# Two-layer graph network with top-p attention: fewer candidates in step two, and the order of the work between the steps

## The chip, the cores and the metric

The kernel runs on one core of a Trainium2 chip. The time is device microseconds of the whole program, so lower is better. Engines are named as in the profile: PE (TensorE, matmuls), DVE (VectorE), ACT (ScalarE), POOL (GpSimd), SP (SyncE, which here only issues DMAs). "L749" is line 749 of the kernel before.

## What is computed

`x` is 2708 x 256 and `adj` 2708 x 2708, with ones in about 0.3% of its places and on its diagonal, each times a number from 0.05 to 1. All is float32. Two layers follow each other:

```python
def adj_layer(x, adj, weight, bias):                  # layer 0
    return relu(concat([x, adj @ x], 1) @ weight + bias)

def top_p(X):                                         # attention of layer 1
    logits = (X @ W1.T @ W2.T) @ (X @ W3.T).T
    probs = softmax(logits)
    # keep, row by row, the largest entries until their sum reaches 0.9
    A = probs * mask
    return A / A.sum(-1)

def layer1(X, S):
    R = S + eye;  R = R / R.sum(-1)
    Z, Xf, Xa = 0, X, X
    for n in range(2):                                # the two steps
        Xf, Xa = R @ Xf, top_p(Xa) @ Xa
        Z = Z + Xf @ U1[n].T + Xa @ U2[n].T
    return layernorm(X + Z) * g + b

x = layernorm(x + adj_layer(x, adj, weight, bias))
x = layernorm(x + layer1(x, adj))
```

## The kernel before, in words

Rows are cut into NB = 22 blocks of 128 (the last, EDGE, has 20). The program has four stages.

**Load and layer 0.** SP loads `xT` in chunks of 512 columns and then the adjacency of block 0. PE makes `y0 = x @ w0` block by block (L392); ACT and DVE copy every other block out of PSUM (L395, L399), and ACT also issues the loads of the weights in between (L397). Then for each of 22 blocks PE multiplies the adjacency with y0 (L257), and DVE does relu and layer norm. DVE also writes down for every block which 128-wide rows of the adjacency hold an entry; sorted lists of these names go through DRAM (`list_d`) and come back as the index tile `ix`, CC = 7 indices for each of 128 lanes and each block. Since a list may be short, the DRAM lists are first filled with the name of an empty row (L279 to L282): an iota writes 154 numbers into `ix` on 128 partitions, and two DMAs of POOL's queue spread them, 28 B a piece.

**Step one.** For each block: logits, exponential, the 64 largest entries in order (`extract1`, candidates from 16 segments of 170 columns), a mask by the threshold, transposes (L527), and the product with x1 (L564). The edge block's product lies in four strips of 32 partitions that `edge_sum` adds with one small matmul (L244). `step1_out` gives three functions that scale the result, turn it (`turn_out`) and project it to the queries and keys of step two and to `za` (`project`, L699).

**Between the steps.** A *y pair* (`ya_pair`, L672 and L675) is four matmuls of two blocks of the turned results with U2, and one copy by ACT into `ya`, through one of the two `acc` buffers of PSUM. There are 11 pairs, and step two's attention products read `ya`. An *R unit* is one matmul (L749) of the product R @ y: 8 units are one R block, 7 with a gathered `y` and one with the block's own rows. `r_units(n)` issues the next n units; when it begins an R block, it also issues the loads of the one after it (`r_load`, SP: adjacency and own rows; POOL: 7 indirect DMAs, L719, into one of two `yg` buffers). A finished R block's `r_out` (L777 in the first half, L792 in the second) is put in a list that is run two slots later. The first half, 22 blocks, reads `yf_d` and writes `v_d`; the second half reads `v_d`. The second half's first gather is issued by the last `r_out` of the first.

**Step two** is a software pipeline of 24 periods, each with six slots g = 0 to 5. In period `per`, DVE searches and cuts: for block `per` it makes `last_level`, one pass over the whole row that keeps what is below the level (`below_level`, L1023), and the eight largest of each segment (`candidates`, L1030, 20 segments of 136); for block `per - 1` it puts the 48 largest candidates in order (`in_order`, L1039 and L1042: MAX8 and MATCH_REPLACE8 in turn), finds the threshold (`threshold`), marks ties (`mark`, four L1083) and cuts the row (`mask`, L1088). ACT makes the exponentials of block `per + 2` (L844, L848) and four passes over block `per + 1` (`try_act`, L966 and L969), whose output goes to a scratch row `scr` that nobody reads. The sums of these passes set the next level by the constants STEPS and FEW. PE turns and multiplies block `per - 2` (L527, L564), makes logits (L507) and the R units that the table `units` gives to the period. `final_slot` does the last layer norms for up to two new blocks and two that had their first norm: `new` ones get their statistics, a slot later are normalized by ACT (L1192) and on POOL multiplied with g and added to x1 (L1207, L1208); they are then `finals` and get their second statistics (L1182). In period 22 and after it the last block ends the program. A sum of flags at the end sends the program through a general path if any row's candidates did not suffice.

The order of the work on each engine is the order in which the Python code issues it. Each engine takes its instructions in that order; an instruction waits until its data are there and its buffer is free, and what stands behind it waits too.

Step two has five rows of exponentials: e0 to e3 are the buffers of step one (`es`), and e4 is half of `tile2`, which takes the place of `xaT_all` (tag "V"), so it can be written only when the last y pair has read that. The other half of `tile2` is `scr`. `tile1` (`low`, `w`) takes the place of x1.

Of the kernel before, what the change touches and what calls it, by code (L numbers as in the profile page):

```python
# [9 lines left out]
FP = mybir.dt.float32  # L10
I32 = mybir.dt.int32
# [9 lines left out]
P = 128  # L21
CH = 512
SEG = 170
NS = 16
SEG2 = 136
NS2 = 20
TOP1 = 64
TOP2 = 48
WS = 4

GUESS = 2.76141059
STEPS = ((0.93339875, 14.44678062, 82.55022771), (0.98700001, 8.00991560, 128.06811957))
FEW = 20.0
TOP_S = 0.8999
TIE_EPS = 1.5e-5
KS = 7
# [1 line left out]
ML = 16  # L40
CW, CC = 128, 7
# [107 lines left out]
def fast_path(ctx, tc, c, flags, fint, xT_d, x_d, w0_d, b0_d, w1_d, w2_d, w3_d, u1_d, u2_d, g_d, b_d):  # L149
    nc = tc.nc  # L150
    N, D, DA, NB, DC, KH, CHS, rows = c.N, c.D, c.DA, c.NB, c.DC, c.KH, c.CHS, c.rows
    ident = c.ident
    adj_d, out_d, x1_d, za_d = c.adj_d, c.out_d, c.x1_d, c.za_d
    NW = SEG * NS
    NF = flags.shape[1]

    big = ctx.enter_context(tc.tile_pool(name="big", bufs=1))
# [11 lines left out]
    def ps_acc(t=None):  # L169
        acc = ps.tile([P, CH], FP, tag="acc", name="acc")  # L170
        if t == NB - 1:
            nc.vector.memset(acc[:, :D + 1], 0.0)
        return acc

    def ps_misc():
        return ps.tile([P, CH], FP, tag="misc", name="misc")
# [56 lines left out]
    fold = small.tile([P, EW], FP, tag="fold", name="fold", bufs=1)  # L233
    nc.vector.tensor_reduce(fold, ident.rearrange("p (j i) -> p i j", i=EW), AX.X, ALU.add)

    def edge_sum(acc, n, stop=True, meanwhile=None):

        p = rows(EDGE)
        four = work.tile([P, 4, P], FP, tag="wT", name="four", bufs=3).rearrange("p k i -> p (k i)")
        nc.scalar.copy(four[:, :n], acc[:, :n])  # L240
        if meanwhile:
            meanwhile()
        whole = ps_misc() if meanwhile else ps_acc()
        nc.tensor.matmul(whole[:p, :n], lhsT=fold[:, :p], rhs=four[:, :n], start=True, stop=stop)  # L244
        return whole

# [18 lines left out]
    LAST = NB * P * NB - 1  # L265
# [11 lines left out]
    for y_d in (c.yf_d, c.v_d):  # L277
        nc.gpsimd.dma_start(out=y_d[rows(NB - 1):, NB - 1, :], in_=zero)
    ix = small.tile([P, NB, CC], I32, tag="ix", name="ix", bufs=1)  # L279
    nc.gpsimd.iota(ix.rearrange("p m c -> p (m c)"), pattern=[[0, NB * CC]], base=LAST, channel_multiplier=0)  # L280
    for i, (a, b) in enumerate(((0, ML), (ML, NB))):
        nc.gpsimd.dma_start(out=c.list_ds[i][:, :CW * CC].rearrange("m (p c) -> p m c", c=CC), in_=ix[:, a:b, :])  # L282
    before_m = small.tile([NB, 1], FP, tag="before_m", name="before_m", bufs=1)
    nc.gpsimd.iota(before_m, pattern=[[0, 1]], base=0, channel_multiplier=KS * CAP,
                   allow_small_or_imprecise_dtypes=True)
# [376 lines left out]
    def ya_pair():  # L662


        if not y_pairs:
            return
        t0 = y_pairs.pop(0)
        pz = ps_acc().rearrange("p (s d) -> p s d", d=D)
        for s in range(2):
            p, at = rows(t0 + s), (t0 + s) * P  # L670
            for j in range(DC):
                nc.tensor.matmul(pz[:p, s, :], lhsT=xaT_all[:, j, at:at + p], rhs=c.u2[:, j, 1, :],  # L672
                                 start=j == 0, stop=j == DC - 1)
        if rows(t0 + 1) == P:
            nc.scalar.copy(ya[:, t0:t0 + 2, :], pz)  # L675
            return
        for s in range(2):
            nc.scalar.copy(ya[:rows(t0 + s), t0 + s, :], pz[:rows(t0 + s), s, :])
# [218 lines left out]
    for t in range(NB):  # L897
        acc = ps_acc(t)
        part = exps1(t + 2) if t + 2 < NB else None
        b = None  # L900
        if t >= NB - 3:
            b = blocks[t - (NB - 3)] = Block(t - (NB - 3))
        ra_next = finish1(t + 1) if t + 1 < NB else None
        for g in range(NG):
            turn(t, g, x1, acc, es[t % 4])
            if ends and 1 <= g <= 3:
                ends[g - 1]()
            if g < NL and t + 3 < NB:
                logits1(t + 3, g)
            if b and g in (0, 2):  # L910
                lg = logits(1, b.t, g // 2)
                if g == 0:
                    shift(b, lg[0])
            if b and g in (1, 3):
                exps2(b, g // 2, *lg)
            if part and g in (3, 4):
                part(g - 3)
            products(1)
            if stores and stores[0][0] <= NG * t + g:
                adj_store(*stores.pop(0)[1:])  # L920
            if g == 2:
                if t + 3 < NB:
                    extract1(t + 3)
                if t < 9:
                    lists.take(2 * t + 2, 2 * t + 4)
                if t == 8:
                    lists.end()
            if (t, g) in at:
                adj_gather(at[t, g])
                stores += [(NG * t + g + i, at[t, g], i - 4) for i in (4, 5)]  # L930
            if (t, g) in y_at:
                name_y()
                y_load(0, y_at[t, g])
            if (t, g) == (NB - 1, 2):
                a_load(0)
        if t == EDGE:
            products(0)
            acc = edge_sum(acc, D, meanwhile=ya_pair)
        ends = step1_out(t, acc, ra)
        ra = ra_next  # L940
    assert not stores and not staged and not to_turn
    r_load(0, 0)
    for f in ends:
        ya_pair()
        f()
    ya_pair()
    for t in range(3):
        exps2(blocks[t], 2, *logits(1, t, 2))
        ya_pair()
    while y_pairs:  # L950
        ya_pair()

    tile1 = big.tile([P, 2 * NW], FP, tag="x1", name="w")
    low = tile1[:, :NW]
    w = tile1[:, NW:]
    tile2 = big.tile([P, 2 * NW], FP, tag="V", name="e4")
    nc.gpsimd.memset(tile2[:, N:NW], 0.0)
    ring.append(tile2[:, :NW])
    scr = tile2[:, NW:]

    def try_act(b, k, part):

# [261 lines left out]
    def final_slot(i):  # L1224


        if i == 2:
            while ready and len(new) < 2:
                new.append(Final(*ready.pop(0)))
                new[-1].load()  # L1230
        if i == 1:
            while done:
                done.pop().store()
        n = len(new) + len(finals)
        if i == 3:
            for k, f in enumerate(new + finals):
                f.stats(k)
        if i == 5 and n:
            roots(0, n)
        if i == 0 and n:  # L1240
            over(0, n)
            for f in finals:
                f.end()
            for f in new:
                f.middle()
            done[:] = finals
            finals[:] = new
            new.clear()
# [3 lines left out]

    each = NB * (CC + 1)
    first = 2 * (CC + 1)
    units = {0: CC + 1, 1: CC + 1}
    rest = each - first - sum(units.values())
    units.update({p: rest * (p - 1) // 8 - rest * (p - 2) // 8 for p in range(2, 10)})
    units.update({p: each * (p - 10) // 11 - each * (p - 11) // 11 for p in range(11, 22)})
    assert first + sum(units.values()) == 2 * each


    b0, b1, b2 = (blocks[t] for t in range(3))
# [7 lines left out]
    try_act(b0, 1, 0)  # L1270
    next_level(b0, 1)
    for per in range(NB + 2):
        if per == NB + 1:
            tail.append(True)
        n_r = units.get(per, 0)
# [8 lines left out]
        for g in range(NG):  # L1284
# [26 lines left out]
            if b_act:  # L1311
                for k, part in {0: ((0, 0),), 1: ((0, 1), (0, 2), (0, 3)), 2: ((1, 0),), 3: ((1, 1), (1, 2), (1, 3))}.get(g, ()):
                    try_act(b_act, k, part)
            next(vector)
            if g == 0:
                final_slot(0)
# [415 lines left out]
```

## Time and profile before

| | |
|---|---|
| median of 3 runs | 1303.6 us (1302.28 to 1304.17) |
| the profiled execution | 1308.28 us, its span 1306.5 us, mean granted clock of PE 0.98 |
| busy: PE, DVE, ACT, POOL | 1236.7, 997.3, 735.6, 641.9 us |
| first adjacency product (L257) of block 0 | 33.2 us |
| last product of step one (L561) | ends at 730.0 us |
| first R unit of step two's stage (L749) | 756.7 us |
| pass L1023 of blocks 0, 1, 2 and 10 | 760.8, 783.7, 794.2, 985.0 us |
| mask L1088 of blocks 20 and 21 | 1267.2, 1282.6 us |

In lines of the timeline the first number is the start in us from the start of the span, the second the duration, then engine, line, operation and what it writes and reads; in brackets stands how long the engine was idle before it, and what released it. In lines of the chain of waits the two numbers are start and duration. A wait that the profile names "issue" has nothing to show for it. PE's instructions appear twice for each matmul of float32 ("x8" is four matmuls), and its busy time is modelled. The granted clock falls to one half in stretches.

### The profile page before, as it was taken

To read this page: it belongs to the slowest core of one execution; us is meant where nothing else is said; L and a number is where in the kernel's file an instruction comes from. 1 tells how busy PE (TensorE), PEld (TensorE's weight loads), DVE (VectorE), ACT (ScalarE), POOL (GpSimd) and SP (SyncE) were. 2 spreads that over 40 slices of the span, in tenths; PEclk is the share of its full clock that TensorE was granted. 3 is DMA by queue.
4 is the path that set the end of the run, shared out by engine and by line. 5 is a ranking of instruction groups with operands and counts; after the bars stand their busy time and mean duration, and the time that the engine had idled before them with its cause. 6 is when DMAs were issued, how large, how long until landed. Compare 5 with 4: busy or idle time off the path is not lost.

```text
span 1306.5 us, 18895 instructions
## 1 busy us (share of the span) xinstructions
PE 1236.7 (95%) x5764; PEld 892.9 (68%) x5764; DVE 997.3 (76%) x3406; ACT 735.6 (56%) x1337; POOL 641.9 (49%) x594
## 2 busy tenths in 40 slices
PE   7999999979899999999999978999999999999975
PEld 5878778843477777777777556777765777766753
DVE  2455445884999997977771279989888999999996
ACT  1010110125456656655665488887888989989821
POOL 1000000002465442577666068878775778888850
PEclk9999999999999999999999888999999999999898
DMA  7455445423322220132324145565663645555551
GB/s 189 152 171 165 149 160 169 148 89 105 119 81 84 70 71 12 40 93 92 91 85 107 49 150 156 177 184 169 185 145 114 197 143 161 175 169 156 151 121 38
DMA packets 101704, 166.00 MB, mean 127 GB/s; under 512 B 17362, under 2 KB 74070, under 8 KB 101594
## 3 DMA queue, kind: packets, MB, share of 16 engines
q1 hardware_dynamic: 75308, 108.65, 26.0%
q0 software_dynamic: 20544, 51.17, 15.1%
q10 hardware_dynamic: 5742, 4.89, 1.4%
q8 instruction: 48, 0.79, 0.3%
q14 instruction: 62, 0.51, 0.1%
HBM read 130.74 MB, written 33.90 MB: 126 GB/s over the span
## 4 chain that ended last, share of the span: by engine, by line
PE 77%; DVE 10%; ACT 6%; DMA 3%; POOL 2%; issue 1%; SPq 0%; ACTq 0%; POOLq 0%; DVEq 0%
PE acc L564 26%; PE acc L257 16%; PE lg L507 9%; PE misc L749 9%; PE tr L527 7%; PE acc L651 2%; DVE e L1088 2%; DVE w L1083 2%; PE acc L462 2%; PE misc L426 2%; PE acc L672 2%; PE misc L699 2%; DMA xT<-in_xT 1%; POOL yg L719 1%; ACT e L844 1%
## 5 line engine op out<-in xcount | busy, mean ns | idle before, releaser
L530 ACT COPY wT<-tr 128x512 f32<-128x512 f32 (+2 forms) x258 | 132.0, 519 | 216.8 <-PE tr L527 215.8
L564 PE MATMUL acc<-x,wT 128*128 128x256 f32 (+1 forms) x924 | 230.5, 388 | 0.0
L564 PE MATMUL acc<-ya,wT 128*128 128x256 f32 (+1 forms) x924 | 228.1, 386 | 0.0
L719 POOL DMA_INDIRECT yg<-v_d,ix x154 | 196.6, 1277 | 59.8 <-issue 23.2
L719 POOL DMA_INDIRECT yg<-yf_d,ix x154 | 191.6, 1244 | 48.3 <-issue 23.1
L564 PEld LDWEIGHTS acc<-x,wT 128*128 128x128 f32 (+1 forms) x924 | 165.2, 189 | 71.0 <-issue 37.4
L257 PE MATMUL acc<-y,adj_t 128*128 128x257 f32 (+1 forms) x924 | 208.4, 381 | 0.0
L564 PEld LDWEIGHTS acc<-ya,wT 128*128 128x128 f32 (+1 forms) x924 | 170.6, 191 | 44.5 <-issue 24.0
L749 PE MATMUL misc<-yg,adj_t 128*128 128x256 f32 (+1 forms) x704 | 185.1, 396 | 14.0 <-DMA yg<-v_d,ix 6.6
L257 PEld LDWEIGHTS acc<-y,adj_t 128*128 128x128 f32 (+1 forms) x924 | 171.8, 189 | 32.7 <-issue 8.9
L367 POOL DMA_INDIRECT adj_t<-in_adj,ix x154 | 167.8, 1089 | 51.8 <-issue 44.1
L749 PEld LDWEIGHTS misc<-yg,adj_t 128*128 128x128 f32 (+1 forms) x704 | 124.2, 191 | 67.2 <-issue 21.5
L507 PE MATMUL lg<-k,q 64*128 64x512 f32 (+3 forms) x528 | 150.2, 596 | 14.0 <-ACT e L848 7.0
L527 PE MATMUL tr<-ident,e 128*128 128x128 f32 (+2 forms) x946 | 148.5, 276 | 7.5 <-DVE e L1088 6.3
L527 PEld LDWEIGHTS tr<-ident,e 128*128 128x128 f32 (+2 forms) x946 | 113.0, 140 | 52.1 <-issue 24.0
L334 POOL DMA_DIRECT2D part_d<-e x1 | 0.6, 573 | 290.3 <-DVE e L333 290.3
L966 ACT ACTIVATE e<-e,st 128x2708 f32<-128x2708 f32 (+1 forms) x43 | 113.5, 2640 | 0.1
L439 ACT COPY x1T<-tr 128x256 f32<-128x256 f32 (+1 forms) x22 | 8.0, 364 | 186.6 <-PE tr L438 186.6
L969 ACT ACTIVATE e<-e,st 128x2708 f32<-128x2708 f32 (+1 forms) x42 | 110.9, 2641 | 0.1
L570 DVE MAX8 cand<-e 128x8 f32<-128x170 f32 (+1 forms) x352 | 87.2, 317 | 26.6 <-ACT e L514 26.6
L1030 DVE MAX8 cand<-w 128x8 f32<-128x136 f32 (+1 forms) x440 | 105.9, 284 | 0.0
L1083 DVE MATCH_REPLACE8 w<-part,e 128x680 f32<-128x680 f32 (+1 forms) x88 | 74.3, 850 | 0.0
(238 smaller groups left out, 1732.3 us busy)
## 6 DMA issues: line engine op xcount, KB each, us to landing
adj_t<-in_adj SPq DMA_DIRECT2D x44, 704.0 KB
adj_t<-adjc_d SPq DMA_DIRECT2D x44, 448.0 KB
adjc_d<-adj_t SPq DMA_DIRECT2D x22, 256.0 KB
base<-za_d SPq DMA_DIRECT2D x40, 128.0 KB
adjc_d<-adj_t SPq DMA_DIRECT2D x22, 192.0 KB
xt<-in_x ACTq DMA_DIRECT2D x21, 128.0 KB
x_d<-x SPq DMA_DIRECT2D x21, 128.0 KB
x1b_d<-xb SPq DMA_DIRECT2D x21, 128.0 KB
```

What stands on the lines that cost most here:

```text
L257: nc.tensor.matmul(acc[:p, :n], lhsT=halves[k // KH][:kw, k % KH, :p], rhs=y[:kw, k, :n], start=k == 0, stop=stop and k == NB - 1)
L367: nc.gpsimd.indirect_dma_start(out=a[:CW, i, :], out_offset=None, in_=adj_rows, in_offset=bass.IndirectOffsetOnAxis(ap=ix[:CW, m, i:i + 1] ...
L507: nc.tensor.matmul(lg[:p, h, :b - a], lhsT=q[o, t * P:t * P + p], rhs=keys[s][o, i, :b - a], start=True, stop=True)
L527: nc.tensor.transpose(tr[:kw, k % 4, :p], e[:p, k * P:k * P + kw], ident[:p, :p])
L530: nc.scalar.copy(wT[:, :full, :p], tr[:, :full, :p])
L564: nc.tensor.matmul(acc[:p, :D], lhsT=wT[:kw, k % 4, :p], rhs=y[:kw, k, :], start=k == 0, stop=k == NB - 1)
L719: nc.gpsimd.indirect_dma_start(out=y[:CW, i, :], out_offset=None, in_=rows_d, in_offset=bass.IndirectOffsetOnAxis(ap=ix[:CW, m, i:i + 1], ...
L749: nc.tensor.matmul(acc[:p, :D], lhsT=a[:kw, k, :p], rhs=y[:kw, k, :], start=k == 0, stop=k == CC)
L966: nc.scalar.activation(scr[:b.p, :N], e, AF.Relu, bias=b.nz, scale=b.l[k], accum_out=b.relu)
L969: nc.scalar.activation(scr[:b.p, :N], e, AF.Sign, bias=b.nz, scale=b.l[k], accum_out=b.sign)
L1030: nc.vector.max(b.cand[:p, 8 * i:8 * i + 8], low[:p, SEG2 * i:SEG2 * (i + 1)])
L1083: nc.vector.match_replace(w[:b.p, W * i:W * (i + 1)], b.part[:b.p, i, :], e2(b.t)[:b.p, W * i:W * (i + 1)], 3.0e38)
```

## The change

Five edits are made together.

1. **Candidates**: 16 segments of 170 columns instead of 20 of 136, 40 in order instead of 48, and other constants for the levels.
2. **The fill of the lists** is made of one iota over 896 columns in 16 partitions of the buffer e2 and goes out in whole rows of 3584 B; `ix` is no longer written for it.
3. **Between the steps** no y pair stands in the edge block's chain, between the three functions of `ends` or between the exponentials; all 11 go to period 0 of step two, two in each slot behind ACT's passes. 8 R units (R block 2) follow them in the slots 3 to 5 of period 0, none in slot 0 to 2; period 1 has 16 units instead of 8, and periods 2 to 9 have 17 instead of 18.
4. **`tile2`** is made at the start of period 1 (`fifth`); until then `scr` is e1, which is free after step one. So ACT's pass over block 0 does not wait for the y pairs.
5. **Statistics of `finals`** are taken in slot 4 instead of slot 3.

```diff
-SEG2 = 136
-NS2 = 20
+SEG2 = 170
+NS2 = 16
 TOP1 = 64
-TOP2 = 48
+TOP2 = 40
...
-STEPS = ((0.93339875, 14.44678062, 82.55022771), (0.98700001, 8.00991560, 128.06811957))
-FEW = 20.0
+STEPS = ((0.97048, 13.37709, 72.87486), (1.01755, 9.09506, 145.60103))
+FEW = 17.8171
...
-    def edge_sum(acc, n, stop=True, meanwhile=None):
+    def edge_sum(acc, n, stop=True):
...
-        if meanwhile:
-            meanwhile()
-        whole = ps_misc() if meanwhile else ps_acc()
+        whole = ps_acc()
...
-    nc.gpsimd.iota(ix.rearrange("p m c -> p (m c)"), pattern=[[0, NB * CC]], base=LAST, channel_multiplier=0)
+    fill = es[2][:max(ML, NB - ML), :CW * CC].bitcast(I32)
+    nc.gpsimd.iota(fill, pattern=[[0, CW * CC]], base=LAST, channel_multiplier=0)
     for i, (a, b) in enumerate(((0, ML), (ML, NB))):
-        nc.gpsimd.dma_start(out=c.list_ds[i][:, :CW * CC].rearrange("m (p c) -> p m c", c=CC), in_=ix[:, a:b, :])
+        nc.gpsimd.dma_start(out=c.list_ds[i][:, :CW * CC], in_=fill[:b - a])
...
-            acc = edge_sum(acc, D, meanwhile=ya_pair)
+            acc = edge_sum(acc, D)
...
     for f in ends:
-        ya_pair()
         f()
-    ya_pair()
     for t in range(3):
         exps2(blocks[t], 2, *logits(1, t, 2))
-        ya_pair()
-    while y_pairs:
-        ya_pair()
...
-    tile2 = big.tile([P, 2 * NW], FP, tag="V", name="e4")
-    nc.gpsimd.memset(tile2[:, N:NW], 0.0)
-    ring.append(tile2[:, :NW])
-    scr = tile2[:, NW:]
+    scr = es[1]
+
+    def fifth():
+        nonlocal scr
+        tile2 = big.tile([P, 2 * NW], FP, tag="V", name="e4")
+        nc.gpsimd.memset(tile2[:, N:NW], 0.0)
+        ring.append(tile2[:, :NW])
+        scr = tile2[:, NW:]
...
         if i == 3:
-            for k, f in enumerate(new + finals):
+            for k, f in enumerate(new):
                 f.stats(k)
+        if i == 4:
+            for k, f in enumerate(finals):
+                f.stats(len(new) + k)
...
-    units = {0: CC + 1, 1: CC + 1}
-    rest = each - first - sum(units.values())
+    units = {0: 0, 1: 2 * (CC + 1)}
+    rest = each - first - (CC + 1) - sum(units.values())
...
     for per in range(NB + 2):
+        if per == 1:
+            fifth()
...
+            if per == 0:
+                ya_pair()
+                ya_pair()
+                r_units((CC + 1) * max(0, g - 2) // 3 - (CC + 1) * max(0, g - 3) // 3)
             next(vector)
```

More of the change, by code (lines that the diff above doesn't have):

```diff
@@ L1254, in fast_path @@
     first = 2 * (CC + 1)
-    units = {0: CC + 1, 1: CC + 1}
-    rest = each - first - sum(units.values())
+    units = {0: 0, 1: 2 * (CC + 1)}
+    rest = each - first - (CC + 1) - sum(units.values())
     units.update({p: rest * (p - 1) // 8 - rest * (p - 2) // 8 for p in range(2, 10)})
     units.update({p: each * (p - 10) // 11 - each * (p - 11) // 11 for p in range(11, 22)})
-    assert first + sum(units.values()) == 2 * each
+    assert first + (CC + 1) + sum(units.values()) == 2 * each
     b0, b1, b2 = (blocks[t] for t in range(3))
```

## The prediction, made before the change was run

> **What bounds the kernel now.** I read the page's forty slices first, then the timeline of single engines, the chain of waits, and last the DMA view of the first microseconds. The slices show PE and DVE busy throughout step two (from 757 us) and POOL at only 7 or 8 tenths. That digit misleads:
>
> ```profile
> 829.27 0.95 POOL L719 DMA_INDIRECT yg<-yf_d,ix  x1 [0.30 <-issue]
> 830.52 0.95 POOL L719 DMA_INDIRECT yg<-yf_d,ix  x1 [0.30 <-PE tr L527]
> 831.77 0.95 POOL L719 DMA_INDIRECT yg<-yf_d,ix  x1 [0.30 <-PE misc L749]
> 833.02 3.59 POOL L719 DMA_INDIRECT yg<-yf_d,ix  x1 [0.30 <-issue]
> ```
> ```profile
> 832.75 3.04 DVE L1088 SCALAR_TENSOR_TENSOR e<-w,st,e 128x2720 f32<-128x2720 f32 x1
> ```
>
> Gathers of y follow each other at 0.95 + 0.30 = 1.25 us, and one takes 3.59 us when a DVE pass over the whole row (L1088, also L1023) runs. So POOL needs per period of the second half (two R blocks) 14 x 1.25 + 2 x 2.4 + 4 x 0.8 = 25.5 us. Its waits between 1005 and 1262 us hold one real one; the rest are the 0.3 us between issues:
>
> ```profile
> POOL yg L719 <- issue: 21.3, 70, 0.3
> ...
> POOL yg L1207 <- ACT yg L1192: 2.6, 1, 2.6
> ```
>
> From 1109 to 1260 the first L1207 of each period comes every 25.1 us. POOL sets the pace there, and DVE shows it by waiting for POOL's layer norm (columns: total, times, longest):
>
> ```profile
> DVE bst L1182 <- POOL yg L1208: 6.5, 10, 0.9
> ```
>
> In the first half (blocks 816 to 910) PE's chain has almost no gap: a period of 23.7 us holds 22 products x 0.433, 22 turns x 0.11, logits 3.2 and 18 R units x 0.433, some 23.1. Between 910 and 985 the gathers fall behind and periods grow to 25.3, 24.2 and 25.2.
>
> Between the steps everything queues behind the y pairs:
>
> ```profile
> 755.86 0.11 POOL L957 MEMSET e<- 128x12 f32 x1 [40.22 <-PE acc L672]
> ...
> 756.31 2.65 ACT L966 ACTIVATE e<-e,st 128x2708 f32<-128x2708 f32 x1
> ```
>
> At the start the chain waits for xT, while DMA throughput collapses (40 parts of 45 us, 1.1 us each):
>
> ```profile
> 3.44 16.70 DMA xT<-in_xT
> 21.16 9.85 PE misc L392 x36
> ```
> ```profile
> GB/s 0 22 190 392 355 377 396 403 240 71 45 78 100 137 157 204 262 278 407 426 392 342 167 35 8 0 0 0 0 0 121 10 0 0 60 225 355 0 0 0
> ```
>
> The fall from about 400 to 45 GB/s at 10 to 14 us is when the two list_d fills (issued 4.4 to 6.5, 77 KB in pieces of 28 B) are served.
>
> **What the Trainium skill says.** "SBUF — State Buffer", section "SBUF: two separate sides", says that DVE and GpSimd share an exclusive port pair and that a blocked GpSimd can't write the descriptors of its DMAs; the 3.59 against 0.95 us agrees. "DMA: Bandwidth & Descriptors", "Specifications", says that pieces under 512 B cost a read-modify-write; the 45 GB/s agrees. "TensorE: Matmul & The Clock Gate", Part 1, says an idle array drops to half rate; ten R records took 4.48 us at 788.6 against 1.30 for six when busy, which agrees.
>
> **The change, part by part** (times on the clock of the old trace).
>
> *Start.* The fill becomes 22 rows of 3584 B; I take its load on the DMA engines as nothing. Before the collapse y0 blocks came every 0.86 us (copies 9.84 to 16.74); then PE waited for xT and for ScalarE, stuck in a load issue, and ran slow after the gap; the last copy is at 31.03. At 0.86 throughout it is at 16.74 + 11 x 0.86 = 26.2. Next is the adjacency load: about 5 MB at 0.39 MB/us is in at 17, so PE stays the bound. **-4.8 us**; bounds 0 (xT late for another reason) and -5.5. Layer 0 is PE's (138.6 of 140 busy), so it carries through.
>
> *Between the steps.* The last products end at 730.0. With no pairs between, the edge chain is copy 0.37, fold 0.6, scale 0.46, turn 0.5, projections 0.5 + 0.5 + 1.0: logits of block 0 at 733.8. Three rounds of logits 1.1 and exponential 1.0 end at 740.0, and after one more logits the first 16 R units run 741.2 to 748.1 (before: to 763.9). ScalarE's pass over block 0 starts at 741 (756.3), DVE's pass L1023 of block 0 at 746.8 (760.8). So 14 us are won first. The cost is in period 0: 11 pairs x 1.75 and 8 R units x 0.433 are 22.8 us on PE, and 11 copies x 0.6 go into ScalarE's queue behind its four passes of 2.83 us. With two acc buffers a pair waits for the copy two pairs back: pairs 1 and 2 end at 751.6, their copies at 752.3; the next pass holds copies 3 and 4 to 757.4, so pairs 5 and 6 end at 760.3, 7 and 8 at 764.2, 9 and 10 at 769.5, pair 11 behind three R units at 772.5. So the last R unit ends at 773.8 and ScalarE at 773.2 (before 772.8). R block 2's r_out (L777) is queued on DVE two slots later, behind period 1's threshold: DVE is there at 761 and **waits until 773.8**, with the marks, the mask and L1023 of block 1 behind it. Before, L777 ran at 775.5 without a wait. ScalarE's work of period 1 is unchanged, 17.6 us, so block 2's levels come at 791 (791.8 before). Of the 14 us, **0 remains** at period 2; bounds -8 (ScalarE's copies fit in the holes) and +4 (PE cold). The e4 memset moves behind POOL's gather of R block 3, ahead of block 4's; that gather needs R block 2 read, later than the last pair, so it costs nothing. SP's loads for R block 1 come earlier, at 735, with nothing due.
>
> *R ahead by a block.* The gather of block 5 starts at about 776 to 785, not 790.3, so POOL has slack. Periods 2 to 9 have 17 R units, not 18: 8 x 0.433 = 3.5, and the starved last three periods fall from 74.7 to 3 x 23.7 = 71.1: 3.6. **-7 us**; bounds -2 and -10.
>
> *DVE's candidates.* 16 MAX8 of 170 took 3.79 us in step one against 4.11 for 20 of 136; ordering at 128 columns goes by 0.72 a round in step one, so 4 x 0.72 + 0.29 = 3.17 against 4.15; the threshold's narrower rows save 0.17. 1.5 us a block, 32 us of DVE. In periods 2 to 9 PE covers it, in 11 to 20 POOL does: the stall goes to POOL's gathers and PE waits for those. It counts where POOL isn't yet full: the 2.6 us wait at 1058 goes. **-2 us**; bounds 0 and -5.
>
> *Stats of the finals a slot later* put two marks (1.7 us) and an h (0.4) ahead of DVE's wait for POOL. POOL hides this until its last gather, 1258.8. In the tail both count: 2.1, and 1.2 for ordering block 21. **-3.3 us**; bounds -1 and -4. STEPS and FEW are numbers only: nothing.
>
> Sum -4.8 + 0 - 7 - 2 - 3.3 = -17.1. The profiled execution goes from 1308.28 (span 1306.5) to 1291; the median of the runs is 4.7 lower than the profiled one, so 1303.6 - 17 = **1287**.
>
> **The rivals.**
> *Only the ends gain*: POOL stays full from period 0 on, so R's earlier start is lost waiting for the buffers of blocks 2 and 3. For it: only 0.3 us gaps from 758 to 976. Against: POOL then starts its chain earlier. Start and tail alone: 1303.6 - 8.1 = 1295.5.
> *The 14 us stay*: ScalarE's copies fit beside its passes and DVE's wait is short. For it: ScalarE has holes of 1 to 2 us there. Against: the sum of PE's work. With another 10 us: 1277.
> *A cold array (slower)*: with the pairs gone PE is half idle from 730 to 741, and drops to half clock as at 788. Each us cold costs half a us of PE, on which ScalarE, DVE and POOL now all wait in period 0. It decides from 34 us of cold between 737 and 795 (it was about 14 before, clock 0.82 from 757 to 796). Cold for 44: 1287 + 22 = 1309.
> *It does not do what it says*: one row whose threshold lies past 40 candidates raises a flag and the general path runs: 27 rounds x 22 blocks x 2 steps x 3.04 us is over 3600 us more.
>
> **Chances.** Forecast 0.57 (own range 1281 to 1293), ends alone 0.20, 14 us stay 0.15, cold 0.05, general path 0.01, two parts failing together near no change 0.02. Faster, same and slower by 0.2% (2.6 us, what a measurement can tell): 0.92, 0.02, 0.06. Leaving out half of the 1277 case, the cold, the general path and no change (0.155) gives 1279 to 1298; the bounds of the single terms reach no further unless two meet.
>
> **What would show it.** Start: the first L257 near 28.4 instead of 33.2 and no fall in GB/s. Between: L966 of block 0 near 741 and R's first L749 near 741, but DVE idle some 12 us ahead of L777 in period 1, and L1023 of block 2 about as far from step one's end as before. First half: L1023 of block 10 some 7 us nearer to it. Second half: L1207 still every 25 us. Tail: last L1207 of the row of full periods to the end 3 us shorter. Wrong if the period of the second half falls towards 23 us (then DVE was the bound), or if period 1 starts before 765.

## The result, and the profile after

The median falls from 1303.42 us (1300.42 to 1304.71, 8 runs) to **1299.18 us** (1298.02 to 1301.70, 8 runs): ratio 0.9972, interval 0.9961 to 0.9983. The medians lie 4.2 us apart. The forecast was 1287 us, with a range of 1279 to 1298: the direction was right, the size a quarter of it. The profiled execution of the changed kernel took 1299.18 us, its span 1297.4. New line numbers: R units L748, R's read L776, DVE's passes L1021 and L1086, gathers L718, layer norms on POOL L1205 and L1206, DVE's statistics of finals L1180, ScalarE's pass L964, products of layer 0 L255.

The start looks as forecast. The chain of waits no longer names xT, the DMA throughput no longer falls, and the first L255 comes at 28.44 us (columns of the chain: start, duration):

```profile
0.75 3.58 DMA e<-in_w
4.38 3.79 PE misc L391 x8
...
8.61 17.66 PE misc L391 x80
```
```profile
GB/s 0 24 206 397 393 387 405 399 402 388 416 421 403 413 402 255 58 1 81 36 0 0 0 0 0 15 113 4 0 0 0 0 225 380 35 0 0 0 4 166
```

Between the steps ScalarE's pass over block 0 starts 18.7 us earlier than in the profile before (737.64 against 756.31; 3.2 us of it lie ahead of step one's end), and DVE then waits for R block 2, as the prediction said. It is read 46.7 us after step one's last product, which ends at 726.8 here and at 730.0 in the profile before (forecast: 773.8 on that clock, 43.8 us after it):

```profile
737.64 2.64 ACT L964 ACTIVATE e<-e,st 128x2708 f32<-128x2708 f32 x1
```
```profile
773.52 0.48 DVE L776 SCALAR_TENSOR_TENSOR base<-misc,rinv,base 128x256 f32<-128x256 f32 x1 [15.44 <-PE misc L748]
```

In the second half POOL keeps the pace of 25 us (first L1205 at 1076.9, 1102.0, 1127.2, 1152.2, 1176.3, 1201.0), and DVE waits longer for it than before (9.7 us in eight times from 1053 to 1253; before, 5.7 in nine from 1060 to 1262):

```profile
DVE bst L1180 <- POOL yg L1206: 9.7, 8, 2.7
```

From profile to profile that reads like a gain of 9 us. It is not one: the execution of the kernel before that was profiled lies 4.9 us over that kernel's median.

### The profile page after: what moved, and what is told of

It reads as the page before. It is cut to its first block, busy times and chain, and to the rows that moved or that the text cites. A ratio compares the mean times of both kernels' runs of the same rounds, so it can differ in the third digit from the quotient of the medians.

```text
span 1297.4 us, 18736 instructions
## 1 busy us (share of the span) xinstructions
PE 1232.0 (95%) x5764; PEld 891.8 (69%) x5764; DVE 974.5 (75%) x3252; ACT 735.1 (57%) x1337; POOL 634.7 (49%) x594
## 4 chain that ended last, share of the span: by engine, by line
PE 79%; DVE 7%; ACT 5%; DMA 4%; issue 2%; POOL 2%; ACTq 0%; POOLq 0%; DVEq 0%
PE acc L563 27%; PE acc L255 16%; PE lg L506 9%; PE misc L748 8%; PE tr L526 7%; DMA yg<-v_d,ix 3%; PE acc L650 2%; PE acc L461 2%; PE misc L425 2%; PE misc L391 2%; PE misc L698 2%; DVE e L1086 1%; POOL yg L718 1%; DMA yg<-yf_d,ix 1%; PE acc L671 1%
## 5 line engine op out<-in xcount | busy, mean ns | idle before, releaser
L718 POOL DMA_INDIRECT yg<-yf_d,ix x154 | 188.5, 1224 | 75.5 <-PE misc L748 38.1
L718 POOL DMA_INDIRECT yg<-v_d,ix x154 | 194.0, 1260 | 61.6 <-issue 22.7
L255 PE MATMUL acc<-y,adj_t 128*128 128x257 f32 (+1 forms) x924 | 210.1, 384 | 0.0
L255 PEld LDWEIGHTS acc<-y,adj_t 128*128 128x128 f32 (+1 forms) x924 | 173.0, 190 | 33.2 <-issue 8.9
L748 PE MATMUL misc<-yg,adj_t 128*128 128x256 f32 (+1 forms) x704 | 182.0, 391 | 11.8 <-DMA yg<-v_d,ix 9.0
L748 PEld LDWEIGHTS misc<-yg,adj_t 128*128 128x128 f32 (+1 forms) x704 | 122.9, 188 | 63.9 <-issue 25.3
L964 ACT ACTIVATE e<-e,st 128x2708 f32<-128x2708 f32 (+1 forms) x43 | 113.5, 2640 | 0.0
L1028 DVE MAX8 cand<-w 128x8 f32<-128x170 f32 (+1 forms) x352 | 94.2, 322 | 0.0
```

What stands on the lines that cost most here:

```text
L255: nc.tensor.matmul(acc[:p, :n], lhsT=halves[k // KH][:kw, k % KH, :p], rhs=y[:kw, k, :n], start=k == 0, stop=stop and k == NB - 1)
L718: nc.gpsimd.indirect_dma_start(out=y[:CW, i, :], out_offset=None, in_=rows_d, in_offset=bass.IndirectOffsetOnAxis(ap=ix[:CW, m, i:i + 1], ...
L748: nc.tensor.matmul(acc[:p, :D], lhsT=a[:kw, k, :p], rhs=y[:kw, k, :], start=k == 0, stop=k == CC)
L964: nc.scalar.activation(scr[:b.p, :N], e, AF.Relu, bias=b.nz, scale=b.l[k], accum_out=b.relu)
L1028: nc.vector.max(b.cand[:p, 8 * i:8 * i + 8], low[:p, SEG2 * i:SEG2 * (i + 1)])
```

## The experiments

Each run is compared with runs of the kernel before on its own chip. To take the start out, the table counts from the end of step one's last product (us; one profile each; "again" is the kernel before once more). The columns for blocks 2, 4 and 10 give the start of DVE's pass L1023 over that block; "last pair" is the first L1207 of the last row of full periods.

| | pass over block 2 | block 4 | block 10 | last pair of L1205 | last DVE instruction | ratio to before |
|---|---|---|---|---|---|---|
| again | 64.2 | 109.0 | 254.4 | 529.2 | 570.5 | 1.0004 |
| candidates alone | 63.6 | 107.4 | 252.2 | 525.5 | 564.7 | 0.9962 |
| all but the part between the steps | 63.5 | 107.4 | 251.4 | 523.8 | 561.1 | 0.9928 |
| the change | 65.5 | 111.4 | 252.0 | 524.2 | 563.0 | 0.9972 |
| the change, padded | 67.7 | 113.5 | 254.0 | 526.1 | 565.0 | 0.9938 |
| R block 2 late | 64.2 | 110.3 | 254.5 | 527.3 | 564.6 | 0.9958 |
| the mix | 62.1 | 106.6 | 247.2 | 519.0 | 557.8 | 0.9877 |
| the mix, R block 2 late | 61.4 | 107.9 | 251.8 | 524.2 | 561.4 | 0.9920 |

How far can a row be trusted? The kernel before (twice), the fill alone and the statistics alone do the same work in step two up to the last pair, the slot of the statistics apart; their four profiles agree within 0.3 us at block 2, 1.4 at block 4, 1.8 at block 10 and at the last pair, and within 0.3 in the distance from block 10 to the last pair. PE's clock may be a part of this. At the end of the program it makes a step of its own: the last 44 products of the edge block take 4.94 us in some executions and 3.30 in others. These are the changed kernel and the change without its part between the steps:

```profile
1276.78 4.94 PE acc L549 x44
```
```profile
1273.92 3.30 PE L551 MATMUL acc<-ya,wT 128*20 128x256 f32 x44 [0.60 <-ACT wT L547]
```

It is not the edits that do it: the padded kernel has 4.94 us in one profile and 3.30 in another. In the last column the rows "candidates alone", "all but the part between the steps" and the two with R block 2 late have the short form, the others the long one, so 1.6 us of a difference between them belongs to no edit.

### The start: the kernel before again, and the fill alone

> The kernel before, unchanged, profiled once more. If the execution that the prediction was read from was a long one (1308.28 us against a median of 1303.4), this profile is some 5 us shorter, and the shortage sits in one place that the prediction counted as a gain (the last three periods of the first half, 74.7 us, or a stretch at half clock). If the profile was typical, the periods are the same to 0.5 us. The times are the same as before within 0.1%.

```diff
-    nc.gpsimd.iota(ix.rearrange("p m c -> p (m c)"), pattern=[[0, NB * CC]], base=LAST, channel_multiplier=0)
+    fill = es[2][:max(ML, NB - ML), :CW * CC].bitcast(I32)
+    nc.gpsimd.iota(fill, pattern=[[0, CW * CC]], base=LAST, channel_multiplier=0)
     for i, (a, b) in enumerate(((0, ML), (ML, NB))):
-        nc.gpsimd.dma_start(out=c.list_ds[i][:, :CW * CC].rearrange("m (p c) -> p m c", c=CC), in_=ix[:, a:b, :])
+        nc.gpsimd.dma_start(out=c.list_ds[i][:, :CW * CC], in_=fill[:b - a])
```

> Only the fill of the lists in whole rows. Theory: layer 0 starts 4.7 us earlier and loses 1.6 of it again to a half-clock stretch in block 0, so about -3 us in all, if what follows carries it to the end. Rival: POOL's chain in step two is set from elsewhere and takes it back: no change.

The kernel before again: 1304.28 us, ratio 1.0004 (0.9996 to 1.0013). The fill alone: 1302.78, ratio 1.0001 (0.9992 to 1.0010). **The fill is worth nothing that can be measured.** The second profile of the kernel before shows why; these are its DMA throughput and its chain from 0 to 45 us:

```profile
GB/s 0 14 210 395 397 379 403 394 202 104 60 35 114 197 210 271 208 378 413 405 387 282 26 0 0 0 52 77 2 0 0 0 65 275 300 0 0 0 0 75
```
```profile
3.30 14.45 DMA xT<-in_xT
...
18.76 8.16 PE misc L392 x36
...
29.09 11.63 PE acc L257 x44
```

The throughput collapses here too, to 35 GB/s. But xT is in at 17.75 us instead of 20.14, PE does the remaining 36 products in 8.16 us instead of 9.85, and L257 starts at 29.1, not 33.2. PE catches up all but some 0.6 us (last copy of y0 at 26.94; in the changed kernel 26.29). The profile that the prediction was made from was a late execution at just this place. The other profiles agree. Of the runs that take about 1300 us, five more with the old fill end step one at 723.7 to 727.5 us, and eight with the new fill at 723.9 to 727.3; the prediction's profile ends it at 730.0. So "again" is 3.0 us shorter for its start, and not, as expected, for the periods of step two: from step one's end on the two profiles differ by 0.5 us.

### The candidates alone

```diff
-SEG2 = 136
-NS2 = 20
+SEG2 = 170
+NS2 = 16
...
-TOP2 = 48
+TOP2 = 40
```
(with STEPS and FEW.)

> Only 16 segments, 40 in order and the constants. Theory (POOL sets the second half, PE the first): DVE is 30 us less busy, the time falls by 0 to 3 us, and L1207 in the second half still comes every 25 us. Rival (DVE sets the second half): 10 periods x 1.5 us = -15 us.

1298.42 us, ratio 0.9962 (0.9948 to 0.9976): 5 us, more than expected, and as much as the whole change. The period of the second half stays at 25 us, so the rival of -15 us falls. By the table, 2.2 us are there at block 10 and 1.5 more at the last L1207. The tail's own part is small: from the last L1207 to the mask of block 21 it is 22.6 us, against 22.9.

### The later statistics alone

```diff
-            for k, f in enumerate(new + finals):
+            for k, f in enumerate(new):
                 f.stats(k)
+        if i == 4:
+            for k, f in enumerate(finals):
+                f.stats(len(new) + k)
```

> Of the change only that the statistics of the finals come a slot later. The prediction gives it 2.1 us in the tail (two marks and an h no longer behind the wait for POOL). Theory now: the masks of blocks 20 and 21 come 2.1 us earlier against the last L1207, but the end waits for PE's turns and products of block 20, so the median falls by less than 1 us. Rival (the prediction): 2.1 us, 1301.3.

1299.13 us, ratio 0.9973 (0.9965 to 0.9981), 3.5 us. The expectation's theory, that PE hides the gain, falls; the prediction's 2.1 us is nearer, and below the interval of the run (2.5 to 4.6 us). The mask of block 20 starts 5.4 us after the last L1207 (kernel before: 7.4), and that of block 21 20.8 us after it (22.9):

```profile
1258.66 3.05 DVE L1088 SCALAR_TENSOR_TENSOR e<-w,st,e 128x2720 f32<-128x2720 f32 x1
```

### Who sets the second half

```diff
-        for i in range(CC):
+        for i in range(CC - 2 * s):
```

> The kernel before, but each R block of the second half gathers only 5 of its 7 index columns: the gathers of two columns are left out, and their products read what the buffer held. POOL's work falls by 4 x 1.25 = 5 us a period; PE, DVE and ACT do the same as before. Theory of the prediction (POOL's queue of 25.5 us sets the 25.1 us of the second half): the period falls to what PE needs, 23 to 23.5 us, some 15 us over nine periods. Rival (DVE, busy 97.7 of 100 us there, sets it): the period stays at 24.5 us or more, so at most 5 us.

> The changed kernel, with the gathers of the same two columns of each R block of the second half left out (their products read what the buffer held). POOL theory: the period falls from 24.9 to 23 or 23.5 us, as in the kernel before. Rival (DVE sets both, 1.5 us a block less here): about 1.5 us shorter a period than the kernel before with the same gathers left out, so 23 against 24.5. If both fall to the same period, DVE's saved work is free time in the second half, and the candidates' gain there must come from how POOL is blocked or from the first half and the tail.

Both kernels leave out two of the seven gathers of each R block in the second half, so they compute something else and serve for their times alone. 1290.41 us, ratio 0.9891 (0.9875 to 0.9907), and 1287.77, ratio 0.9879 (0.9856 to 0.9902). The period falls to 23.2 us in both, in the kernel before as in the changed one: the first L1207 of a period comes at 1079.7, 1102.9, 1126.1, 1149.3, and POOL now waits for ScalarE. Windows and POOL's timeline of the kernel before without the two gathers (columns of the first line: window, its length, busy us of PE, PEld, DVE, ACT, POOL, clock, DMA share, GB/s):

```profile
1079.70:1172.50 92.80, 92.74 (x442) 68.55 (x441) 91.21 (x339) 89.22 (x157) 59.22 (x57) 1.00 0.51 159
```
```profile
1102.87 0.73 POOL L1207 TENSOR_TENSOR yg<-yg,gb 128x256 f32<-128x256 f32 x1 [5.35 <-ACT yg L1192]
```

PE is busy for all of it. POOL's queue was the bound, PE lies 1.9 us a period behind it. DVE is nearly as full here (91.21 us), but with the fewer candidates of the changed kernel the period is the same, so DVE's share of the change is slack and the rival, a bound by DVE, falls. How the candidates alone still won 1.5 us in this half isn't shown.

### Between the steps: alone, left out, and R block 2 moved

> Only the order between the steps (y pairs in period 0, R's first blocks early, scr in e1). Theory: period 2 begins at the same distance from the end of step one or 1 to 2 us later, as DVE waits some 13 us for R block 2 in period 1; then the starved periods 8 to 10 of the first half shrink, 2 to 4 us in all: -1 to -3 us. Rival (the 14 us stay): -10 us or more.

Edits 3 and 4 alone: 1305.37 us, ratio 1.0008 (0.9999 to 1.0017), of which 2.1 us are a gap at the program's end that is treated last.

> The change without its part between the steps: candidates, fill of the lists and the later statistics of the finals. Theory (between the steps and R's earlier start give 4 to 5 us away by period 2 and win them back by period 9, so they are worth nothing; the gap of 2.2 us at the end comes with them): as the padded kernel within 1.5 us, near 1297, and no gap at the end (5.5 us from the last DVE instruction). Rival (R ahead is worth what the prediction said, 7 us): 1300 or above.

Edits 1, 2 and 5: 1292.76 us, ratio 0.9928 (0.9915 to 0.9942), against 0.9938 for the changed kernel without that gap ("padded": it has one store more, see the last experiment). So the part is no gain. The table says how: against the candidates alone the changed kernel is 1.9 us late at block 2 and 4.0 late at block 4, and wins 4.2 back from there to block 10. The windows of 12 us behind step one's last product show where PE's time goes. First the kernel before (again):

```profile
727.50:739.50 12.00, 12.00 (x56) 8.74 (x56) 0.41 (x1) 4.01 (x11) 0.00 (x0) 1.00 0.06 11
739.50:751.50 12.00, 12.00 (x52) 8.38 (x51) 9.23 (x24) 5.25 (x12) 0.00 (x0) 1.00 0.31 100
751.50:763.50 12.00, 11.46 (x50) 8.01 (x48) 6.27 (x18) 10.59 (x16) 7.16 (x7) 1.00 0.40 118
763.50:775.50 12.00, 8.12 (x22) 4.98 (x22) 11.44 (x51) 11.80 (x18) 9.04 (x10) 0.72 0.66 202
```

and the changed kernel:

```profile
726.80:738.80 12.00, 7.65 (x27) 2.62 (x28) 6.12 (x19) 5.31 (x13) 0.00 (x0) 0.84 0.36 111
738.80:750.80 12.00, 12.00 (x50) 9.59 (x47) 10.78 (x28) 5.27 (x8) 7.99 (x6) 0.87 0.32 92
750.80:762.80 12.00, 10.51 (x48) 8.72 (x48) 6.79 (x34) 11.02 (x14) 7.94 (x9) 1.00 0.65 216
762.80:774.80 12.00, 11.42 (x52) 8.95 (x51) 1.28 (x4) 6.59 (x17) 1.83 (x3) 1.00 0.05 6
```

Before, the pairs kept PE full and at full clock in the first 24 us. Now PE does 7.65 us of work in the first 12 and runs in part at half clock (0.84, 0.87; R's first 32 records took 8.18 us, against 7.17). What it didn't do there it does from 763 to 775, while DVE stands still (1.28 us busy). Six such windows, 72 us, hold 60.0 us of busy PE in the kernel before (again) and 58.7 in the change, which by then has also done 5 R units more (46 against 41), so less of the rest. Behind them PE is all but full in both, so work that is left over there comes out as delay. More time at half clock is not the reason: of these 72 us the change spends 10.2 so, the kernel before 13.7. The same wait of DVE can be moved:

```diff
     units = {0: 0, 1: 2 * (CC + 1)}
-    rest = each - first - (CC + 1) - sum(units.values())
+    rest = each - first - sum(units.values())
...
-                r_units((CC + 1) * max(0, g - 2) // 3 - (CC + 1) * max(0, g - 3) // 3)
```

> The padded changed kernel, but R block 2 is not in period 0 behind the y pairs: period 1 keeps 16 units (now R blocks 2 and 3), periods 2 to 9 have 18 as in the kernel before. Theory A (DVE's 15.4 us wait for L776 of R block 2 is what gave the 14 us back): the wait is gone, L1021 of block 1 comes near 771 instead of 781.7, L1021 of block 2 some 4 us nearer to step one's end than in the changed kernel (65.5 us there); over periods 2 to 9 the 8 extra units take 3.5 us back, so the time is that of the padded kernel within 1.5 us. Rival B (ScalarE's copies and PE's work hold period 1 in any case): block 2 keeps its distance of 65 us, and the time is 3 to 4 us longer than the padded kernel's.

1297.83 us, ratio 0.9958 (0.9942 to 0.9974). The 15 us wait ahead of block 1 is gone, and the pass over block 1 comes 39.0 us after step one instead of 54.9. Block 2 gains only 1.3 us on the changed kernel (3.5 on the padded one), since DVE stands a little later, for R and then for the exponentials that ScalarE could only begin behind the last copy:

```profile
773.84 0.48 DVE L777 SCALAR_TENSOR_TENSOR base<-misc,rinv,base 128x256 f32<-128x256 f32 x1 [7.65 <-PE misc L749]
...
782.23 0.16 DVE L852 TENSOR_REDUCE bulk<-st 128x1 f32<-128x3 f32 x1 [4.11 <-ACT e L844]
```

So DVE's wait was the symptom. Rival B fits block 2 better. For the time, the median (0.8 us above the padded kernel's) and the last pair (1.2 later) fit theory A, while the ratios lie 2.6 us apart with intervals that overlap; the time doesn't decide between the two.

### The mix: three pairs back where PE idles

```diff
     for t in range(3):
         exps2(blocks[t], 2, *logits(1, t, 2))
+        ya_pair()
```

> The padded changed kernel with three of the 11 y pairs put back between the steps, one behind each of the three exponentials, where the trace of the changed kernel shows PE idle for about 1 us each (PE busy 7.65 of the first 12 us behind step one). Eight pairs are left for period 0. Theory (the sum of PE's work, 22.8 us, ends period 0): three pairs of 1.75 us less there, at 0.6 us of copy each in ScalarE's queue between; R block 2 is read some 3 to 4 us nearer to step one's end than the 48.9 us of the padded kernel, L1022 of block 2 about as much, and the median falls by 2 to 3 us, to 1294 or 1295. Rival (ScalarE's passes and copies end it): L1022 of block 2 keeps its distance of 67.7 us, the first R unit comes 2 us later, and the median is 1297 to 1298.

> The three pairs put back between the steps, together with R block 2 moved out of period 0 (period 1 has 16 units, periods 2 to 9 have 18). If both edits act on PE's sum in period 0 they add: block 2's pass L1022 some 3 us nearer than the 64.2 us that the late R block 2 gave alone, and 3.5 us lost again over periods 2 to 9, so the median is within 1 us of the mix alone. If ScalarE's work of period 1 decides (it starts when the last copy is out), the late R block 2 gives nothing more at block 2 and the median is 2 to 3 us above the mix.

The mix takes **1285.93 us**, ratio 0.9877 (0.9858 to 0.9895); with R block 2 late as well 1293.39, ratio 0.9920 (0.9901 to 0.9940). In the mix PE does 10.71 of the first 12 us, R's first 32 records take 7.17 us, and DVE's wait shrinks:

```profile
724.70:736.70 12.00, 10.71 (x33) 5.46 (x34) 4.84 (x12) 3.92 (x11) 0.00 (x0) 0.72 0.34 111
```
```profile
768.32 0.48 DVE L777 SCALAR_TENSOR_TENSOR base<-misc,rinv,base 128x256 f32<-128x256 f32 x1 [9.24 <-PE misc L749]
```

Block 2 comes 5.6 us nearer than in the padded kernel, and the last L1207 7.1: the theory's direction at twice its size. A part of this is the clock, since in the 72 us behind step one the padded execution ran at half clock for 20.5 us, the mix for 13.7. Two comparisons are free of that. Against the changed kernel, whose execution had only 10.2 us of it, the mix still wins 3.4 us at block 2 and 5.2 at the last L1207. And where R block 2 is late in both, with 13.7 us at half clock in each, the three pairs bring 2.8 us at block 2 and 3.1 at the last L1207, while PE's busy time in the 72 us rises from 57.4 to 61.0 us. So filling PE's idle time is worth some 3 to 5 us.

From the mix to the mix with R block 2 late, block 2 comes only 0.7 us nearer still, but 5.2 us are lost by the last L1207, so its expectation's second case holds, and by more than it said. That is what R's lead of a block is worth once the start of step two no longer pays for it.

The median fell by more than the traces do, and on another chip. In the next six runs the kernel before itself takes 1346 us (1338 to 1358), and the engines also stand still with nothing in the profile to show for it (ScalarE 22.1 us, DVE 16.3 us at one line each from 300 to 730 us of the padded kernel), so only ratios among these six count. That it was the chip, as two of the expectations have it, isn't shown: the record gives the number 5 for the chip of runs at 1304 us and for that of the last two at 1346.

> The padded changed kernel once more, on the same chip and against the same runs of the kernel before as the next one, since what the part between the steps is worth is read from the two. Theory (the part gives 4 us away up to period 3 and wins as much back by period 9): within 1.5 us of the change without that part. Rival (it is a net loss): 3 us or more above it.

> The change without its part between the steps, once more. Theory: within 1.5 us of the padded changed kernel. Rival: 3 us or more below it.

> As the mix, but two y pairs behind each of the three exponentials: six between the steps, five left for period 0. If the mix won because PE's idle time between the steps was filled, the second pair of each place finds no idle time (one needs 1.75 us, the hole is about 1 us): the first R unit comes 4 to 5 us later, period 0 ends at the same distance from step one's end, and the median is that of the mix or up to 2 us more. If it won because fewer copies stand in ScalarE's queue in period 0, it gains once more, 2 us or more below the mix.

```diff
             if per == 0:
-                ya_pair()
-                ya_pair()
+                ya_pair(nc.vector.tensor_copy)
+                ya_pair(nc.vector.tensor_copy)
```
(moved behind `next(vector)`, and `ya_pair` uses the copy that it is given.)

> The mix with the copies of the eight y pairs of period 0 made by DVE, behind its work of the slot, instead of ScalarE. If ScalarE's queue (eight copies of 0.6 us behind passes of 2.83 us) holds the pairs and the start of period 1's exponentials, ScalarE starts period 1 some 4 us earlier, L1022 of block 2 comes 2 to 4 us nearer to step one's end than the mix's 62.1 us, and the median falls by up to 3 us. If PE's sum holds it, ScalarE only waits longer for the logits and nothing changes; if DVE's own queue holds the copies up, the pairs end later and it is slower by 1 to 3 us.

> The padded changed kernel, beside the mix on one chip, because the chip of the last four runs was slower by 43 us for the kernel before too, so that medians across chips can't be set against each other. Expected: 0.994 of the kernel before.

> The mix (three y pairs between the steps, eight in period 0) beside the padded changed kernel on one chip. Theory (PE's idle time between the steps was what the change lost, 5 to 7 us in the traces): 5 to 8 us below the padded kernel. Rival (the 11 us between the two medians were a difference of chips): within 3 us of it.

| | median | ratio (interval) |
|---|---|---|
| padded change, second run | 1348.02 | 0.9991 (0.9958 to 1.0023) |
| without the part between, second run | 1342.77 | 0.9961 (0.9938 to 0.9984) |
| six pairs between | 1336.22 | 0.9929 (0.9908 to 0.9949) |
| mix with DVE's copies | 1344.63 | 0.9981 (0.9960 to 1.0002) |
| padded change, third run | 1342.61 | 0.9973 (0.9953 to 0.9992) |
| mix, second run | 1335.65 | 0.9931 (0.9908 to 0.9955) |

On one set of runs the mix lies 7.0 us below the padded change: the theory's 5 to 8; the rest of the first 11 us did not come again. The padded change itself missed its expected 0.994. Six pairs do about as well as three (0.9929 and 0.9931, of two sets of runs), so fewer copies in ScalarE's queue bring nothing more. Copies on DVE lose 8 us against the six pairs, more than the third case of the expectation: DVE's queue holds them up, and the last y pair ends 52.6 us behind step one, in the mix of the last set 40.5. Without the part between the steps the median was lower in both comparisons, by 4.3 and 5.3 us, but the first is one across chips and the intervals overlap in both. That the part doesn't win the 7 us of the forecast is shown; that it loses some is likely, not shown.

### The gap at the end of the program

In the changed kernel the last DVE instruction is followed by 7.6 us, before by 5.5. SP, behind the branch over the general path (L129), stands still twice instead of once (columns: total, times, longest):

```profile
SPq L129 <- SPq L129: 4.8, 2, 2.6
```

The kernel run with the part between the steps alone has the same gap, the fill alone, the candidates alone and the statistics alone have not; SP has 941 instructions in the changed kernel and in the one with that part alone, and 942 in the others. One more store on SP, in layer 0 and far from the end, adds to the number:

```diff
-        nc.sync.dma_start(out=c.x1b_d[m * P:m * P + p, :], in_=xb[:p])
+        for lo_, hi_ in ((0, 64), (64, P)) if m == 5 else ((0, p),):
+            nc.sync.dma_start(out=c.x1b_d[m * P + lo_:m * P + hi_, :], in_=xb[lo_:hi_])
```

> The changed kernel with one instruction more on SP: in layer 0 the store of x1b of block 5 goes out as two halves. At the end of the program SP, behind the branch over the general path, runs one semaphore instruction and then stands still for 2.2 us; the kernel before, with one SP instruction more in all (942 against 941), does not. Theory (the place of the branch's target in the instruction stream costs a fetch): with 942 instructions the gap is gone, the last DVE instruction to the end takes 5.5 us instead of 7.6, and the median falls by 2.1 us against the changed kernel, to about 1297. Rival (the gap is a wait for something that the change made late): it stays at 7.6 us and the median at 1299.

1297.07 us, ratio 0.9938 (0.9918 to 0.9957). SP ran 943 instructions here, and the second stop is gone, with 5.5 us to the end:

```profile
SPq L129 <- SPq L129: 2.7, 1, 2.7
```

All seventeen profiles with 942 or 943 SP instructions have the short end, all three with 941 the long one. So the gap hangs on SP's instructions, not on work that came late, which is the same with the store. That it is the place of the branch's target that counts, and that a fetch of instructions fills the gap, is argued, not shown.

## Why the prediction was wrong, step by step

| step | forecast | measured | from |
|---|---|---|---|
| start | -4.8 | -0.5 at most | fill alone: ratio 1.0001; y0 done at 26.29 and 26.94 |
| between the steps | 0 | +4.0 | block 4: 111.4 against 107.4 |
| R ahead by a block | -7 | -4.2 | block 4 to 10: 140.6 against 144.8 |
| candidates, with their part of the tail | -3.2 | -4.0 | 3.7 to the last L1207, 0.3 behind it |
| statistics of finals | -2.1 | -2.1 | masks of blocks 20 and 21 |
| end of the program | none | +2.1 | 7.6 against 5.5 us |
| sum | -17.1 | -4.7 | the runs: -4.2 |

Most numbers in the third column are differences between single profiles, so their sum may be wrong by a us or two. Two steps carry most of the miss: the start, and PE's idle time between the steps.

**The start failed by its base.** "The profiled execution goes from 1308.28 (span 1306.5) to 1291; the median of the runs is 4.7 lower than the profiled one, so 1303.6 - 17" subtracted one delay twice. The profiled execution lay 4.7 us above the median, and its layer 0 began 4.1 us late (33.2 against 29.1 in the second profile, of which 2.5 are left at step one's end); the median never held what the fill was to save. The collapse by the small pieces is real: it stands in both profiles of the kernel before and not in those of the changed kernel and of the fill alone. In the usual execution PE makes up for it all but 0.5 us.

**Between the steps**, "of the 14 us, 0 remains" named the right place and wait, but block 4 comes 4.0 us late. The step that failed is that PE's idle time between the steps was put at nothing. The prediction says itself that "PE's chain has almost no gap" in the first half, and that without the pairs PE is half idle from 730 to 741. It counted that hole only as a question of the clock (the cold array), moved the pairs' 19 us into period 0, and compared DVE's due time alone with the old one, though period 1 also took on 8 more units. Time that PE idles ahead of a stretch that PE fills comes back as delay, and the mix shows it: with three pairs in the hole the last L1207 comes 5.2 us nearer. How the 4.0 us at block 4 divide among PE, ScalarE's copies and DVE's wait isn't shown.

R block 2 was read 2.9 us later than forecast, counted from step one's end (46.7 and 43.8), and DVE waited 15.4 us, not some 12. That delay was there before period 0: R's first unit came 13.0 us behind step one, forecast 11.2, and its first 16 units took 8.2 us, forecast 6.9. The forecast ran them at full speed, with "+4 (PE cold)" as a bound, and PE did drop to half clock beside them. The Trainium skill's page "TensorE: Matmul & The Clock Gate", Part 1, says that the rate is decided in windows of 3.4 us that run free of the kernel; the clock records here agree (half-clock stretches of 3.4 us or a multiple, at other places in each execution, near step one's end in some profiles and not in others).

**R ahead** won 2.8 us less than forecast. "8 x 0.433" counted eight periods as PE's, and the first two aren't. From block 4 to 7 the change's period is 23.5 us and that of the candidates alone 23.9, nearly the forecast's 0.43; and the last three take 70.1 us (forecast 71.1, before 74.7). But blocks 2 to 4 took 43.8 us with the candidates alone, under PE's pace, and 45.9 in the change.

**Right were** POOL as the bound of the second half (shown by the left-out gathers: 25.1 to 23.2 us), DVE's new wait, and the tail's statistics. Why a gather is long beside a pass of DVE, by descriptors that can't be written as the prediction has it or otherwise, no run separates; the trace shows the length (3.59 us against 0.95). The terms of PE's period of 23.7 us add up to 22.9, not 23.1. Of "1.2 for ordering block 21" 0.3 came; what the candidates won ahead of it was nearly twice the forecast.

**The end** stood in no step and no rival. Of the rivals, "only the ends gain" came nearest in time (1295.5), for a wrong reason: the start was no gain. The slower rival, a cold array, needed 34 us at half clock. In the 72 us behind step one the changed kernel spent 10.2 us so, less than the kernel before (13.7), and the padded one 20.5.

## What to carry to other kernels

Before a delay seen in one profiled execution is counted as a gain, ask whether the median holds it: if the profile lies above the median by just that much, it doesn't. When work is moved out of a chain to shorten it, look at what the engine then does in the holes; here three or six of the eleven pairs between the steps, and the rest later, did better than all or none of them. And move a backlog through to the next engine-bound stretch before calling a wait the end of it.

## What the runs showed of the hardware

- Programs with 941 SP instructions ended 7.6 us behind the last DVE instruction, those with 942 or 943 some 5.5 us (three profiles and seventeen).
- PE's half clock in the last 44 edge products made them 4.94 us instead of 3.30, in two executions of the same program (the padded kernel): 1.6 us of the tail that no edit made.
- Whole-kernel times of one program differed by 43 us between earlier and later runs (1303 and 1346 us), with nothing in the profile to explain it.
